# Layer 0 without Sqrt and with one set of ScalarE functions asked for first; layer 1 loads its first image ahead of its weights

## The chip, the core and the metric

The kernel runs on one core of a Trainium2 chip. The metric is the device time of one launch in microseconds (us). TensorE (PE) multiplies matrices, VectorE (DVE), ScalarE (ACT) and GpSimd (POOL) work element by element, SyncE (SP) issues transfers (DMA). Each engine runs its own instructions in the order in which they stand and waits for the others by semaphores. [...] which functions are at hand depends on the set that is loaded, and a load is an instruction of its own in its stream (ACT_TABLE_LOAD in the profile).

## The reference

Four layers, each `x = x + layer(gn(x))` on four images of 64 x 64 points and 128 channels, in fp32. `gn` normalizes groups of 4 channels over an image with `1 / sqrt(var + 1e-5)`. Cut to what matters:

```python
def _gn(v, G=32, eps=1e-5):
    g = v.reshape(B_, H_, W_, G, C_ // G)
    m, s = mean(g), var(g)              # over H, W and the group
    return ((g - m) / jnp.sqrt(s + eps)).reshape(v.shape)
# layer 0: selective scan in four directions
xh, z = split(x @ in_proj_w.T);  z = silu(z)
xc = silu(conv3x3(xh) + conv_b)
delta = softplus(dts + bias);  h = exp(delta * A) * h + delta * u * B;  y = h . C
y = layernorm(y) * z @ out_proj_w.T
# layer 1: Fourier layer
f = irfft(rfft(x, rows)[:16] * w1) + irfft(rfft(x, columns)[:16] * w2)
out = layernorm(relu(f @ ff_w0 + b0) @ ff_w1 + b1)
```

Layer 2 is an attention between Fourier-transformed tokens, layer 3 a windowed attention; neither is touched.

## The kernel before

**Layer 0** (`layer0`, line 83). For each image `before` (line 148) reads it twice in 8 chunks of 512 points: first for the statistics of the group norm (`bn_stats`, line 161, then `group_scale`, lines 64 to 80), then to transpose it (`x_ps`, line 183), normalize it (`xn`), project it to `z` (`zp`, line 198, two matmuls) and convolve it as 9 taps each for two halves of the channels (`cv`, line 206). Each result goes through `silu` (line 217): ScalarE takes Exp of the negated value, Ln of one plus that, Exp of the negated result, and DVE multiplies with the value itself (`e`, line 222), which frees its PSUM bank; four banks go round. The result is written to DRAM, and the convolved one a second time in the order of columns (`xw`, lines 231 to 234). For the first image this runs alone, as an opening; for the next three it is a side work, spread over the scan of the image before.

The scan goes over 128 units (4 images, 4 directions, 8 chunks). A unit has 16 slots, one a state: GpSimd makes `dB` (line 477), ScalarE the decay `dA` (Exp, line 483) for two halves, DVE scans them (`h`, line 484), TensorE transposes `h` (line 371), ScalarE copies it (line 381), TensorE multiplies it with C (line 406). `inputs` (line 294) makes the next unit's `delta`: Exp (line 320), Ln (line 321), a bound on DVE (line 323), and then `du` on GpSimd (line 326). Inside the scan the order of the engines' instructions is that of the program, written out by hand (`manual_schedule`, line 449); outside of it a scheduler orders them.

**Square roots.** `rstd` (line 43) is Sqrt on ScalarE and a reciprocal on DVE. Layer 0 calls it once an image, from `group_scale`, and asks for the set with Exp and Ln behind it (`exp_and_ln`, lines 121 and 164); for the layer norm at its end (`after`, lines 250 to 254) it takes Exp(-0.5 Ln(var + eps)). That request has no data to wait for: outside of the hand-written order it stands at the head of the ScalarE stream as built, not behind the Sqrt.

**Layer 1** (`layer1`, line 716) loads its weights (`layer1_weights`, line 586): `w1` and `w2` on SyncE's queue, 2 MB each, six small ones on ScalarE's, `c_an1` the fifth of them. Then it runs one image after another (`layer1_image`, line 607): the image in four loads of 512 KB (`load_image`, line 709), the group norm's statistics (lines 58 and 59), the row transform with `c_an1` (`pu`, line 631, `U`, line 632), the mixing of modes with `w1` (`pg`, lines 643 and 646), the transform back (`pt`, `ph`), the same along the columns with a second copy of the image (`xa`, line 626) and `w2`, and a two-layer network (`pf`, `po`). Behind its first image the weights of layer 2 are loaded and prepared with short DVE operations (`layer2_weights`, line 732); the scheduler places them among those of the image. Its tiles lie where layer 0's lay, so its loads wait for layer 0's last work.

A DMA reports to one of eight semaphores, shared out in turn over the queues of SyncE and ScalarE, and as built the next DMA on a semaphore is issued only when the one before it has landed.

Of the kernel before, what the change touches and what calls it, by code (L numbers as in the profile page):

```python
# [10 lines left out]
F32 = mybir.dt.float32  # L11
AF = mybir.ActivationFunctionType
# [4 lines left out]
P = 128  # L17
# [3 lines left out]
DM = 128  # L21
NJ = NT // P
# [7 lines left out]
class Shared:  # L30
# [30 lines left out]
                nc.scalar.copy(keep[:, c * CH : (c + 1) * CH], ps)  # L61
        return self.group_scale(st, psum, small, tag)

    def group_scale(self, st, psum, small, tag):
        nc = self.nc
        mv = small.tile([P, 2], F32, name="gn_mv")
        nc.vector.bn_aggr(mv, st)
        gm = psum.tile([P, 1], F32, name="gn_gm", tag=tag)
        nc.tensor.matmul(gm, lhsT=self.gmat, rhs=mv[:, 0:1], start=True, stop=True)
        gms = small.tile([P, 1], F32, name="gn_gms")  # L70
        nc.vector.tensor_copy(gms, gm)
        d = small.tile([P, 1], F32, name="gn_d")
        nc.vector.tensor_tensor(d, mv[:, 0:1], gms, ALU.subtract)
        nc.vector.scalar_tensor_tensor(d, d, d, mv[:, 1:2], ALU.mult, ALU.add)
        gv = psum.tile([P, 1], F32, name="gn_gv", tag=tag)
        nc.tensor.matmul(gv, lhsT=self.gmat, rhs=d, start=True, stop=True)
        s = self.rstd(small, gv, [P, 1], "gn_s")
        o = small.tile([P, 1], F32, name="gn_o")
        nc.vector.scalar_tensor_tensor(o, gms, -1.0, s, ALU.mult, ALU.mult)
        return s, o  # L80


def layer0(sh, A, x_in, x_out, scr):
# [6 lines left out]
    tc, nc = sh.tc, sh.nc  # L90
    with ExitStack() as ctx:
        pool = lambda name, bufs, **kw: ctx.enter_context(tc.tile_pool(name=name, bufs=bufs, **kw))
        wp = pool("l0w", 1)
        tmp = pool("l0tmp", 2)
        small = pool("l0small", 2)
        ps = pool("l0ps", 1, space=PSUM)
        psx = pool("l0psx", 3, space=PSUM)
        psm = pool("l0psm", 1, space=PSUM)
        psy = pool("l0psy", 1, space=PSUM)

        w_in = wp.tile([P, 4, P], F32, name="w_in")
        nc.sync.dma_start(w_in, A["in_proj"].rearrange("i (m d) -> i m d", d=P))
        cols = wp.tile([P, 14], F32, name="cols")
# [14 lines left out]
        for xd in xds:  # L118
            nc.vector.memset(xd, 0.0)
            nc.vector.memset(xd[64:65, :], 1.0)  # L120
        exp_and_ln = lambda: nc.scalar.preload_act_table_set("natural_log_exp_and_others")
        w_out = wp.tile([P, 2, P], F32, name="w_out")
        nc.sync.dma_start(w_out, A["out_proj"].rearrange("(s p) o -> p s o", p=P))

# [23 lines left out]
        def before(b, bank, later):  # L148

            st = small.tile([P, NCH, 6], F32, name="gn_st")
            for c in range(NCH):
                yield "l"
                t = tmp.tile([P, 4, DM], F32, name="xs", tag="t2", bufs=4)
                nc.sync.dma_start(t, tiles(x_in(b)[c * CH : (c + 1) * CH, :]))
                yield "m"
                pt = bank("gn_ps")
                for q in range(4):
                    nc.tensor.transpose(pt[:, q * P : (q + 1) * P], t[:, q, :], sh.ident)  # L160
                later("dve", lambda c=c, pt=pt: nc.vector.bn_stats(st[:, c, :], pt))
            yield "m"
            s_, o_ = sh.group_scale(st, psm, small, "m")
            exp_and_ln()
            for c in range(NCH):
                yield "l"
                r0, r1 = max(8 * c - 1, 0), min(8 * c + 9, 64)
                j0, j1 = r0 // 2, (r1 + 1) // 2
                t = tmp.tile([P, 6, DM], F32, name="xt", bufs=1)
                nc.sync.dma_start(t[:, 0 : j1 - j0], tiles(x_in(b)[j0 * P : j1 * P, :]))  # L170

                xn = tmp.tile([P, 10, 66], F32, name="xn")
                nc.gpsimd.memset(xn[:, :, 0:66:65], 0.0)
                if c == 0:
                    nc.gpsimd.memset(xn[:, 0, :], 0.0)
                if c == NCH - 1:
                    nc.gpsimd.memset(xn[:, 9, :], 0.0)
                for j in range(j0, j1, 3):
                    yield "m"
                    e = min(j + 3, j1)  # L180
                    pt = bank("x_ps")
                    for q in range(j, e):
                        nc.tensor.transpose(pt[:, (q - j) * P : (q - j + 1) * P], t[:, q - j0, :], sh.ident)
                    a, z = max(r0, 2 * j), min(r1, 2 * e)
                    later(
                        "dve",
                        nc.vector.tensor_scalar,
                        xn[:, a - 8 * c + 1 : z - 8 * c + 1, 1:65],
                        pt.rearrange("p (h w) -> p h w", w=64)[:, a - 2 * j : z - 2 * j],
                        s_,  # L190
                        o_,
                        ALU.mult,
                        ALU.add,
                    )
                for s in range(2):
                    yield "z"
                    zp = bank("zp")
                    nc.tensor.matmul(zp, lhsT=w_in[:, 2 + s, :], rhs=xn[:, 1:9, 1:65], start=True, stop=True)
                    silu(zp, 0.0, 0.0, scr(f"z{b % 3}")[s, :, c * CH : (c + 1) * CH], later, (0, 0, 1))
                for s in range(2):  # L200
                    for t in range(9):
                        yield "c"
                        if t == 0:
                            pm = bank("cv")
                        dy, dx = divmod(t, 3)
                        nc.tensor.matmul(  # L206
                            pm,
                            lhsT=taps[:, s, t, :],
                            rhs=xn[:, dy : dy + 8, dx : dx + 64],
                            start=(t == 0),  # L210
                            stop=(t == 8),
                        )
                    bias = conv_b[:, s : s + 1], conv_nb[:, s : s + 1]
                    xo = silu(pm, *bias, scr(f"xr{b % 2}")[s, :, c * CH : (c + 1) * CH], later, (0, 1, 2))
                    later("act0", by_columns, xo, scr(f"xw{b % 2}")[s], c, slots=4)
# [220 lines left out]
        def later(place, f, *a, slots=1, **kw):  # L436

            todo.setdefault((slot + slots, place), []).append(lambda: f(*a, **kw))
# [147 lines left out]
def layer1_weights(sh, A, wp):  # L586
    nc = sh.nc
    w = {}
    for name in ("w1", "w2"):
        w[name] = wp.tile([P, 16, 2, P], F32, name=name)  # L590
        nc.sync.dma_start(w[name], A[name])
    w["ff0"] = wp.tile([P, 4, P], F32, name="ff0")
    nc.scalar.dma_start(w["ff0"], A["ff_w0"].rearrange("i (f k) -> i f k", k=P))
    w["ff1"] = wp.tile([P, 4, P], F32, name="ff1")
    nc.scalar.dma_start(w["ff1"], A["ff_w1"].rearrange("(f k) o -> k f o", k=P))
    w["b0"] = wp.tile([P, 4], F32, name="b0")
    nc.scalar.dma_start(w["b0"], A["ff_b0"])
    w["rows"] = wp.tile([P, 3, P], F32, name="rows1")
    nc.scalar.dma_start(w["rows"], A["l1_rows"].partition_broadcast(P))
    w["an"] = wp.tile([P, 96], F32, name="c_an1")  # L600
    nc.scalar.dma_start(w["an"], A["c_an1"])
    w["sy"] = wp.tile([P, 256], F32, name="c_sy1")
    nc.scalar.dma_start(w["sy"], A["c_sy1"])
    return w


def layer1_image(sh, w, pools, x_dram, x_out):

    nc = sh.nc
    big, tmp, small, ps = pools  # L610
    x = big.tile([P, NJ, DM], F32, name="x1")
    load_image(nc, x, x_dram)
    s_, o_ = sh.group_norm(lambda j: x[:, j, :], ps, small, tag="a")
    o8 = small.tile([P, 1], F32, name="o8")
    nc.vector.tensor_scalar(o8, o_, 8.0, None, ALU.mult)
# [2 lines left out]
    for axis in range(2):  # L618
# [20 lines left out]
        for g in range(4):  # L639
            pg = ps.tile([P, 4, 2, 64], F32, name="pg", tag="b")  # L640
            for q in range(4):
                m = 4 * g + q
# [34 lines left out]
    for c in range(NCH):  # L677
# [14 lines left out]
        st = small.tile([P, 4, 6], F32, name="ln_st")  # L692
# [4 lines left out]
        r = sh.rstd(small, mv[:, :, 1], [P, 4], "ln_r")  # L697
# [11 lines left out]
def load_image(nc, x, x_dram):  # L709
    for q in range(4):  # L710
        nc.sync.dma_start(
            x[:, 8 * q : 8 * q + 8, :], x_dram[1024 * q : 1024 * q + 1024, :].rearrange("(j p) d -> p j d", p=P)
        )


def layer1(sh, A, x_in, x_out, l2w, wt):

    tc, nc = sh.tc, sh.nc
    with ExitStack() as ctx:
        pool = lambda name, bufs, **kw: ctx.enter_context(tc.tile_pool(name=name, bufs=bufs, **kw))  # L720
        pools = pool("l1big", 2), pool("l1tmp", 2), pool("l1small", 2), pool("l1ps", 4, space=PSUM)
        wp = pool("l1w", 1)
        w = layer1_weights(sh, A, wp)
        for b in range(NB):
            layer1_image(sh, w, pools, x_in(b), x_out(b))
            if b == 0:
                setup = pool("l2set", 1)
                later = layer2_weights(sh, A, l2w, setup, pools[3], wt)
        return later
# [1094 lines left out]
```

## Time and profile before

| | |
|---|---|
| time, median of 3 (lowest to highest) | 8356.3 us (8350.7 to 8357.7) |
| span of the profiled run | 8355.5 us |
| busy: PE, DVE, ACT, POOL | 79%, 81%, 76%, 66% |
| opening of layer 0, to the first `du` | 0 to 247.5 us |
| scan and rest of layer 0 | to 6091 us |
| layer 1 | to about 6700 us |
| table loads in layer 0 | 79 of 1283 ns |
| ScalarE in layer 0, the costliest | `dA` 4096 x 690 ns, `hT` 2048 x 1010 ns |
| DVE in layer 0, the costliest | `h` 4096 x 1270 ns |

The page shows the busy share of each engine in 40 slices of 209 us, and the groups of instructions by line, operation and tile, with what ended the idle time before them. The views used below cut out a stretch: the timeline lists instructions in order of time (start, duration, engine, line, operation, out<-in, count, and in brackets the engine's idle time before it with what ended it); the waits sum who waited for whom; the chain of waits follows what ended last back through what released it; the windows give each engine's busy time, TensorE's granted clock and the DMA engines' share and rate in stretches.

### The profile page before, as it was taken

What the parts mean: (1) busy time and instruction counts of PE and PEld (TensorE: products, weight loads), DVE (VectorE), ACT (ScalarE), POOL (GpSimd) and SP (SyncE); (2) the same over time, 40 slices, a digit from 0 to 9 for tenths busy, and PEclk for the clock granted to TensorE, in tenths of its full rate; (3) what the DMA queues carried; (4) which work ended last, traced back from release to release, by engine and by line L of the source; (5) the groups of instructions that cost most, each with busy time, mean ns of one, the idle gap of its engine ahead of it and who ended that gap; (6) DMA issues with size and microseconds to landing.
All of it is one profiled execution on the core that took longest, in us unless ns stands there. A gap on an engine that the chain in (4) does not pass through costs nothing.

```text
span 8355.5 us, 140584 instructions
## 1 busy us (share of the span) xinstructions
PE 6592.1 (79%) x52976; PEld 4182.2 (50%) x52976; DVE 6756.6 (81%) x7952; ACT 6333.0 (76%) x10320; POOL 5485.2 (66%) x2502
## 2 busy tenths in 40 slices
PE   7588888778788777888887777787778978686689
PEld 3344454444445444444544444454457756464456
DVE  2689999998899999889999999999944545645578
ACT  6799999999899889989989999999822213315467
POOL 0689889988888889888888999999800011020233
PEclk9799999999999999999999999999989988788799
DMA  6445555444555554455555445554432041331332
GB/s 111 132 144 179 166 170 173 164 160 156 169 169 177 175 171 153 154 176 159 175 173 175 163 153 181 177 175 169 165 94 52 18 118 38 86 100 31 95 93 78
DMA packets 1281978, 1163.79 MB, mean 139 GB/s; under 512 B 637973, under 2 KB 1075825, under 8 KB 1214354
## 3 DMA queue, kind: packets, MB, share of 16 engines
q1 hardware_dynamic: 1279618, 1153.06, 43.6%
q8 instruction: 417, 6.83, 0.3%
q14 instruction: 263, 2.15, 0.1%
q10 hardware_dynamic: 1680, 1.74, 0.1%
HBM read 962.66 MB, written 189.74 MB: 138 GB/s over the span
## 4 chain that ended last, share of the span: by engine, by line
PE 21%; ACT 11%; DVE 10%; issue 3%; POOL 2%; DMA 2%; SPq 1%; ACTq 0%; DVEq 0%; POOLq 0%
DVE h L484 4%; ACT hT L381 4%; ACT dA L483 4%; PE pt L371 2%; POOL dB L477 1%; PE po L686 1%; PE pf L681 1%; PE pz L872 1%; PE pt L1507 1%; PE pu L872 1%; DVE in_st L872 1%; PE pb L872 1%; PE ps L1561 1%; DVE m L872 1%; PE pa L872 1%
## 5 line engine op out<-in xcount | busy, mean ns | idle before, releaser
L484 DVE TENSOR_TENSOR_SCAN h<-dA,state,dB 128x512 f32<-128x512 f32 x4096 | 4962.0, 1270 | 379.5 <-ACT dA L483 269.8
L477 POOL TENSOR_TENSOR dB<-du,Bb 128x1024 f32<-128x1024 f32 x2048 | 4820.0, 2385 | 567.4 <-DVE h L484 398.0
L371 PE MATMUL pt<-ident,h 128*128 128x128 f32 x16384 | 2256.9, 282 | 1023.1 <-ACT hT L381 1018.9
L371 PEld LDWEIGHTS pt<-ident,h 128*128 128x128 f32 x16384 | 1846.3, 143 | 2063.8 <-ACT hT L381 1815.1
L483 ACT ACTIVATE dA<-delta,A_neg 128x512 f32<-128x512 f32 x4096 | 2745.6, 690 | 157.8 <-DVE h L484 136.7
L381 ACT COPY hT<-pt 128x1024 f32<-128x1024 f32 x2048 | 2068.9, 1010 | 182.5 <-PE pt L371 169.3
L406 PE MATMUL yT<-hT,W 128*32 128x256 f32 x16384 | 1400.9, 415 | 2.7 <-DVE y L422 2.1
L872 POOL COPY XG<-Xs 64x9 f32<-64x9 f32 (+2 forms) x44 | 11.0, 294 | 1024.9 <-ACT Xs L872 1024.9
L406 PEld LDWEIGHTS yT<-hT,W 128*32 128x32 f32 x16384 | 454.3, 150 | 353.6 <-issue 338.4
L206 PE MATMUL cv<-xn,taps 128*128 128x512 f32 x1152 | 620.1, 639 | 8.7 <-DVE e L222 8.7
L1545 POOL TENSOR_TENSOR S<-S,sm 128x784 f32<-128x784 f32 x128 | 191.4, 1495 | 408.2 <-DVE sm L1543 347.3
L317 PE MATMUL dp<-xd,w_dt 65*128 65x512 f32 x512 | 300.0, 669 | 105.4 <-ACT Ct L304 92.0
L326 POOL TENSOR_TENSOR du<-delta,u 128x1024 f32<-128x1024 f32 x128 | 305.1, 2384 | 78.5 <-DVE delta L323 78.5
L206 PEld LDWEIGHTS cv<-xn,taps 128*128 128x128 f32 x1152 | 185.5, 190 | 248.5 <-issue 244.6
L298 PE MATMUL xd_ps<-u,w_x 128*48 128x512 f32 x512 | 251.1, 614 | 44.0 <-DMA u<-l_xw 19.8
L1552 ACT ACTIVATE S<-S,mx 128x196 f32<-128x196 f32 x512 | 227.9, 448 | 32.7 <-DVE mx L1579 32.2
L682 ACT ACTIVATE h<-pf,b 128x512 f32<-128x512 f32 x128 | 88.0, 687 | 145.0 <-PE pf L681 145.0
L323 DVE SCALAR_TENSOR_TENSOR delta<-delta,dp 128x512 f32<-128x512 f32 x256 | 169.3, 661 | 27.7 <-ACT delta L321 27.7
L317 PEld LDWEIGHTS dp<-xd,w_dt 65*128 65x128 f32 x512 | 79.4, 195 | 220.7 <-ACT Ct L304 150.6
L1421 POOL MEMSET kp<- 128x210 f32 (+1 forms) x8 | 1.8, 287 | 275.0 <-DMA x<-m 275.0
L320 ACT ACTIVATE delta<-dp 128x512 f32<-128x512 f32 x256 | 152.4, 595 | 30.1 <-PE dp L317 25.6
L1507 PE MATMUL pt<-ident,S 128*98 128x128 f32 x1024 | 165.2, 285 | 4.4 <-POOL S L1545 1.9
(336 smaller groups left out, 7282.4 us busy)
## 6 DMA issues: line engine op xcount, KB each, us to landing
Bb<-l_B SPq DMA_DIRECT2D x512, 1024.0 KB
W<-l_W SPq DMA_DIRECT2D x512, 256.0 KB
l_y<-y SPq DMA_DIRECT2D x128, 512.0 KB
u<-l_xw SPq DMA_DIRECT2D x64, 512.0 KB
y<-l_y SPq DMA_DIRECT2D x64, 512.0 KB
u<-l_xr SPq DMA_DIRECT2D x64, 512.0 KB
V<-l_v SPq DMA_DIRECT2D x512, 49.0 KB
wr<-wt SPq DMA_DIRECT2D x128, 136.0 KB
```

What stands on the lines that cost most here:

```text
L206: nc.tensor.matmul(pm, lhsT=taps[:, s, t, :], rhs=xn[:, dy : dy + 8, dx : dx + 64], start=(t == 0), stop=(t == 8),)
L298: nc.tensor.matmul(xd_ps, lhsT=w_x[:, s, k, :], rhs=u[:, s, :], start=(s == 0), stop=(s == 1))
L317: nc.tensor.matmul(dp, lhsT=w_dt[:, k, s * P : (s + 1) * P], rhs=xd, start=True, stop=True)
L326: nc.gpsimd.tensor_tensor(du, delta, u, ALU.mult)
L371: nc.tensor.transpose(pt[:, j, s, :], G["h"][:, s, t0 : t0 + 32, :].rearrange("p t n -> p (t n)"), sh.ident)
L381: return lambda: nc.scalar.copy(hT, pt.rearrange("p j s d -> p j (s d)"))
L406: nc.tensor.matmul(U["yT"][e][32 * jo : 32 * jo + 32, qo % 2, :], lhsT=U["Ws"][G["g"]][:, :, 4 * q + j], rhs=hT[:, j, :], start=((e, jo) n ...
L477: nc.gpsimd.tensor_tensor(dB, du, B_now[:, q : q + 1, :].to_broadcast([P, 2, CH]), ALU.mult)
L483: nc.scalar.activation(dA, delta[:, s, :], AF.Exp, scale=A_neg[:, k, s, n : n + 1])
L484: nc.vector.tensor_tensor_scan(h[:, s, :, q], dA, dB[:, s, :], state[:, s, n : n + 1], ALU.mult, ALU.add)
L872: r = f(*args, **kw)
L1507: nc.tensor.transpose(pt[:, half, hp, :], U["S"][:, e, hp, 98 * half : 98 * half + 98], sh.ident)
```

## The change

In layer 0 the square root is replaced by Exp(-0.5 Ln(var + eps)), and the set of functions that has both Exp and Ln is asked for once, ahead of everything else. It is meant to keep ScalarE from switching sets. In layer 1 the first image is loaded ahead of the weights, and the analysis matrix ahead of the other small weights, since the image's statistics and row transform come before the first use of `w1`.

```diff
-    def group_scale(self, st, psum, small, tag):
+    def group_scale(self, st, psum, small, tag, rstd=None):
...
-        s = self.rstd(small, gv, [P, 1], "gn_s")
+        s = (rstd or self.rstd)(small, gv, [P, 1], "gn_s")
...
+        nc.scalar.preload_act_table_set("natural_log_exp_and_others")
         w_in = wp.tile([P, 4, P], F32, name="w_in")
...
-        exp_and_ln = lambda: nc.scalar.preload_act_table_set("natural_log_exp_and_others")
+        def exp_rstd(pool, var, shape, tag):
+            r = pool.tile(shape, F32, name=tag)
+            nc.scalar.activation(r, var, AF.Ln, bias=sh.eps5[: shape[0]])
+            nc.scalar.activation(r, r, AF.Exp, scale=-0.5)
+            return r
...
-            s_, o_ = sh.group_scale(st, psm, small, "m")
-            exp_and_ln()
+            s_, o_ = sh.group_scale(st, psm, small, "m", exp_rstd)
...
 def layer1_weights(sh, A, wp):
     w = {}
+    w["an"] = wp.tile([P, 96], F32, name="c_an1")
+    nc.scalar.dma_start(w["an"], A["c_an1"])
     for name in ("w1", "w2"):
...
-    w["an"] = wp.tile([P, 96], F32, name="c_an1")
-    nc.scalar.dma_start(w["an"], A["c_an1"])
...
-def layer1_image(sh, w, pools, x_dram, x_out):
+def layer1_image(sh, w, pools, x_dram, x_out, x=None):
...
-    x = big.tile([P, NJ, DM], F32, name="x1")
-    load_image(nc, x, x_dram)
+    if x is None:
+        x = big.tile([P, NJ, DM], F32, name="x1")
+        load_image(nc, x, x_dram)
...
+        x = pools[0].tile([P, NJ, DM], F32, name="x1")
+        load_image(nc, x, x_in(0))
         w = layer1_weights(sh, A, wp)
         for b in range(NB):
-            layer1_image(sh, w, pools, x_in(b), x_out(b))
+            layer1_image(sh, w, pools, x_in(b), x_out(b), x if b == 0 else None)
```

## The prediction

> **What bounds the kernel now.** I read the page first (which engine is full in which slice), then the groups of ScalarE for its table loads, then the stretches in which the change lies: the waits and the timeline of layer 0's opening, the timeline of its first scan units, the chain of waits across the change of layer. ACT and DVE are at 8 to 9 tenths from slice 2 to slice 28, so layer 0 from about 250 to 6090 us is paced by the two of them together; before it comes an opening of 250 us, and behind it a stretch in which nothing computes.
>
> The groups of instructions, whole kernel, the rows of the table loads (count | busy us, mean ns | idle before):
>
> ```profile
> L342 ACT ACT_TABLE_LOAD x55 | 70.6, 1283 | 1.0
> ...
> L46 ACT ACT_TABLE_LOAD x8 | 10.3, 1283 | 20.4 <-DMA c_sy<-in_c_sy 20.3
> L321 ACT ACT_TABLE_LOAD x8 | 10.3, 1283 | 0.1
> L483 ACT ACT_TABLE_LOAD x8 | 10.3, 1283 | 0.1
> L121 ACT ACT_TABLE_LOAD x4 | 5.1, 1283 | 0.8 <-PEq L1814 0.7
> ```
>
> Layer 0 holds 79 of these loads (55 + 8 + 8 + 4, and 4 of L46). By windows, 61 lie before 250 us, 18 after: so they cluster where layer 0 opens. The timeline there (start, duration, engine, line, operation, idle before):
>
> ```profile
> 101.22 0.69 ACT L342 ACTIVATE e<-cv,conv_nb 128x512 f32<-128x512 f32 x1
> ...
> 101.92 1.28 ACT L342 ACT_TABLE_LOAD   x1
> ...
> 103.21 0.63 ACT L342 ACTIVATE e<-e 128x512 f32<-128x512 f32 x1
> 103.86 1.28 ACT L342 ACT_TABLE_LOAD   x1
> 105.15 0.63 ACT L342 ACTIVATE e<-e 128x512 f32<-128x512 f32 x1
> 105.81 0.75 DVE L222 SCALAR_TENSOR_TENSOR e<-cv,cols,e 128x512 f32<-128x512 f32 x1 [3.46 <-ACT e L342]
> ...
> 106.71 3.44 PE L206 MATMUL cv<-xn,taps 128*128 128x512 f32 x4 [2.31 <-DVE e L222]
> ```
>
> One silu is Exp, load, Ln, load, Exp, then the product on DVE, which frees the PSUM bank; TensorE waits 2.31 us for that bank. And its first four matmuls then take 0.86 us each, against 14.76 us for 34 (0.43 each) in the chunk before: the wait costs a second time, as a slow clock. The waits of PE from 33 to 250 us:
>
> ```profile
> PE cv L206 <- DVE e L222: 8.7, 4, 2.3
> PE zp L198 <- DVE xn L342: 8.5, 8, 1.8
> PE zp L198 <- DVE e L222: 5.5, 3, 1.8
> ```
>
> So 8.7 + 5.5 = 14.2 us of the opening hang on the silu, 8.5 on something else (xn). In the first scan units (timeline from 268 us) the same pair of loads stands in front of a dA:
>
> ```profile
> 282.43 1.28 ACT L321 ACT_TABLE_LOAD   x1
> ...
> 284.38 1.28 ACT L483 ACT_TABLE_LOAD   x1
> 285.67 0.69 ACT L483 ACTIVATE dA<-delta,A_neg 128x512 f32<-128x512 f32 x1
> ...
> 286.39 1.29 DVE L484 TENSOR_TENSOR_SCAN h<-dA,state,dB 128x512 f32<-128x512 f32 x1 [4.61 <-ACT dA L483]
> ```
>
> Last, the chain of waits from 6080 to 6290 us, where layer 1 begins:
>
> ```profile
> 6097.14 8.71 DMA pa<-in_pa
> 6105.86 6.13 SPq L711
> 6112.04 5.38 SPq L711
> ...
> 6117.46 10.96 DMA x<-x
> ...
> 6133.69 9.54 PE pu L631 x64
> ```
>
> The image is the last to arrive (6128.43), behind w1 and w2, and pg, the first user of w1, starts only at 6144.21.
>
> [...] from the Exp that ends at 101.91 to the Ln that starts at 103.21 a load costs 1.30 us in all, which I use as 1.29. [...] between 401 and 1828 us Exp and Ln alternate with no load. [...] w2's issue waited 9.0 us for b0, a transfer of a few bytes from the ACT queue, which went beside w1's 2 MB.
>
> **The change part by part.**
>
> *Opening of layer 0.* With Sqrt gone and the set asked for ahead of all, nothing in layer 0 needs another set; as built, layer 0 has 1 load in place of 79, and every other instruction of it keeps its place except that a Reciprocal on DVE (0.16 us) becomes an Exp on ACT (about 0.18, as L254's row of the same kind), for four small columns: nothing. Each silu gets 2 x 1.29 = 2.57 us shorter. The largest wait is 2.31, so the bank is free before TensorE asks: with the loads gone, the product would end near 103.9, and PE reaches that cv at 102.41 + 1.99 = 104.4. All 14.2 us go. The four chunks that wait at cv also run slowly: 17.4 us for 36 cv matmuls against 14.76 + 1.02 = 15.8 undisturbed; 4 x 1.6 = 6.4. After the last cv nothing hides the last silu: 2.6. Then the first delta: Exp, load, Ln, DVE, twice in sequence, where the second L483 load of each pair lies beside a matmul or GpSimd's du; 2 x 1.29 = 2.6. Sum 25.8. The waits for xn (8.5) stay. What could take the place: the slots of e and xw. A column write xw takes 7.8 us to land (issued 101.34, ACT freed at 109.16); in the faster rhythm z's second Exp would ask for that slot about as late relative to the write as now, so at most 1 us, off PE's path.
>
> *First scan units.* Six pairs of L321 and L483 loads remain past 250 us. Before 286.39 DVE idles 4.61 us, 2.57 of it the two loads in sequence. As a test: the unit from 290.2 to 341.4 us and the one from 341.4 to 391.8 (two pairs each; from the starts of du) take 51.2 and 50.4 us, those at 493.0, 539.2 and 584.1 take 46.2, 44.9 and 46.0: 5 us for two pairs, the whole price. 6 x 2.57 = 15.4; I take 15.
>
> *The three later group norms* (400, 1834, 3313 us): the load of Sqrt's set lies in ACT's wait for gn_gv (3.3 to 5.1 us) and is free; the one behind Sqrt delays the next dA by 1.3, but the gain is cut by DVE's own gn_o (1.13 us beside GpSimd): 1.0 + 0.7 + 0.7 = 2.4; I take 2.
>
> *Start of layer 1.* Image first, then w1, w2. Its first load takes w1's place at 6093.75. Its third waits for the analysis matrix c_an, now first on the ACT queue, its fourth for ff1, by the semaphores of the build. Before the fourth lands some 3.2 MB must pass: x 2.1, ff0 and ff1 0.5, rows 0.2, c_sy and c_an 0.2, pa and pb 0.3. The next image of the same form ran at 281 to 312 GB/s (windows 6142 to 6148). 3.2 MB at 290 is 11 us from 6095: landed at 6106, against 6128.4. Bounds: x alone, 2.1 MB at 290 and 1 us: 6103; all 3.2 MB at 177 GB/s, the rate beside xa: 6113. From there on the chain is the same length: 5.3 us to gn_s, 10.5 to pg. pg at 6122 finds w1 landed: 2.5 MB more at 385 GB/s (window 6096 to 6098) is 6112.5; in the slow case 6113 + 8 = 6121 against pg at 6129. w2 at 6118, xa (at 177 GB/s, 12 us) at 6130, while its pu comes at 6165 - 22 = 6143. So 22 us. DVE's constants for layer 2 move behind the first axis' hT copies: 13 short operations, some 6 us, in the 7 us of the second pu, so U at L635 is just met; cost 0, at worst 1. The first waits for tok, landed near 6139 and asked for at 6146.
>
> Sum: 25.8 + 15 + 2 + 22 = 65 us; 8356.3 - 65 = 8291.
>
> **The rivals.** (1) *The first layer's gain shrinks to a half*: the 512 B packets of x run at 177 GB/s or tok holds up DVE, and layer 1 wins 10, not 22: 8303. For it: x's own issues took 6.1 and 5.4 us; against: they stood behind w2. 12%. (2) *Transfers become the bound of the opening*: the column writes are many and small, the DMA engines are at 0.54 to 0.72 there; if waits for slots take back 14 + 6, only 5 remain there: 8311. Against it: 3.0 us of such waits in all now. 8%. (3) *Slower*: the scan's units are no steady clockwork (44.9 to 46.2 for like ones); if the shifted phase of ACT against GpSimd and DVE cost 0.7 us in each of 120 units, 84 us, more than the gain: 8375. Nothing in the trace speaks for it but that spread. 2%. (4) *More*: x lands at 6103, PE stays at full clock through pu: 8281. 8%.
>
> **How the numbers follow.** The main case, 70%, with its own bounds (layer 1 15 to 25, opening 21 to 28, units 13 to 16) lies in 8282 to 8303. Rival 1 and half of rivals 2 and 4 are taken in: 8280 to 8312. Faster by over 0.2% (16.7 us) in all cases but (3) and a mixture of (1) and (2): 0.96; same 0.02; slower 0.02.
>
> **What would show it.** One table load before 6090 us; PE's waits for e gone from 33 to 250 us, the waits for xn still near 8; first du near 222 in place of 247.5; units 1 and 2 near 46 us; x landed some 12 us after its first issue, in place of 24 (and 35 after w1's), and pg 16 us later without a wait for w1. Wrong if the waits for e become waits for transfers, if the units stay at 50, or if pg waits for w1.

## The result and the profile after

| | before | after |
|---|---|---|
| time, median (lowest to highest, runs) | 8353.5 us (8348.6 to 8357.7, 4) | 8298.5 us (8295.9 to 8301.2, 4) |
| span of the profiled run | 8355.5 us | 8299.4 us |
| table loads | 99 | 21 |
| first `du` | 247.5 us | 220.7 us |
| last `du` of layer 0 | 5998.3 us | 5949.4 us |
| first `pg` of layer 1 | 6144.2 us | 6087.0 us |

After over before is 0.9934, with a 95% interval from 0.9917 to 0.9952: 55 us faster, where 65 were forecast. A second pair on another chip gave 0.9936 (0.9924 to 0.9949).

The table loads among the groups of ScalarE in the kernel after (count | busy us, mean ns | idle before): one is left for all of layer 0, that of L102; the others belong to the later layers.

```profile
L883 ACT ACT_TABLE_LOAD x12 | 15.4, 1283 | 48.7 <-DVE in_d L883 48.5
L46 ACT ACT_TABLE_LOAD x4 | 5.1, 1283 | 25.9 <-DMA x<-x 25.8
L1563 ACT ACT_TABLE_LOAD x4 | 5.1, 1283 | 0.1
L102 ACT ACT_TABLE_LOAD x1 | 1.3, 1283 | 0.7 <-PEq L1825 0.7
```

The timeline of the opening shows a silu without loads. From Exp to the product on DVE it takes 2.04 us (87.85 to 89.89), 4.59 before (101.22 to 105.81), and TensorE goes on with `cv` under it without a gap:

```profile
83.79 11.75 PE L214 MATMUL cv<-xn,taps 128*128 128x512 f32 x27
...
87.85 0.69 ACT L350 ACTIVATE e<-cv,conv_nb 128x512 f32<-128x512 f32 x1 [4.09 <-PE cv L214]
...
88.57 1.29 ACT L350 ACTIVATE e<-e 128x512 f32<-128x512 f32 x2
...
89.89 0.75 DVE L230 SCALAR_TENSOR_TENSOR e<-cv,cols,e 128x512 f32<-128x512 f32 x1 [5.41 <-ACT e L350]
```

The waits of PE from 33 to 230 us (us in total, times, longest): the two rows that ended at `e` are gone, the one for `xn` is what it was, and no wait for a transfer has come in. The first row, the wait for the last column write, was 19.8 us before and is not new.

```profile
PE xd_ps L306 <- DMA u<-l_xw: 16.8, 1, 16.8
PE zp L206 <- DVE xn L350: 8.6, 8, 1.9
```

In the first scan units the pair of loads between delta and `dA` is gone, and DVE's idle time ahead of the scan falls from 4.61 to 0.31 us:

```profile
294.88 0.60 ACT L328 ACTIVATE delta<-dp 128x512 f32<-128x512 f32 x1
...
295.51 0.64 ACT L329 ACTIVATE delta<-delta 128x512 f32<-128x512 f32 x1
...
296.04 0.68 ACT L491 ACTIVATE dA<-delta,A_neg 128x512 f32<-128x512 f32 x1
...
296.75 1.28 DVE L492 TENSOR_TENSOR_SCAN h<-dA,state,dB 128x512 f32<-128x512 f32 x1 [0.31 <-ACT dA L491]
```

At the change of layer the chain of waits of the kernel after looks different from what was forecast:

```profile
6046.53 6.54 DMA ff<-in_ff_w
6053.08 18.46 DMA x<-x
6071.69 1.95 PE gn_ps L58 x8
...
6076.82 9.24 PE pu L640 x64
...
6087.04 0.69 PE pg L652 x2
```

The image's last quarter, 512 KB, is issued at 6053.08 and lands 18.46 us later, in place of 10.96 us. From the issue of the first quarter (6045.39) it is 26.2 us, where the forecast had some 12. That is where most of the missing time is. `w1`, as forecast, is no wait.

### The profile page after: what moved, and what is told of

The parts are those of the page before. It is cut to its first block, busy times and chain, and to the rows that moved or that the text cites. A ratio compares the mean times of both kernels' runs of the same rounds, so it can differ in the third digit from the quotient of the medians.

```text
span 8299.4 us, 140501 instructions
## 1 busy us (share of the span) xinstructions
PE 6571.5 (79%) x52976; PEld 4171.0 (50%) x52976; DVE 6753.8 (81%) x7948; ACT 6229.0 (75%) x10246; POOL 5482.7 (66%) x2502
## 3 DMA queue, kind: packets, MB, share of 16 engines
q10 hardware_dynamic: 1680, 1.74, 0.1%
## 4 chain that ended last, share of the span: by engine, by line
PE 21%; ACT 11%; DVE 11%; issue 3%; DMA 2%; POOL 2%; SPq 1%; DVEq 0%; ACTq 0%; POOLq 0%
DVE h L492 4%; ACT hT L389 4%; ACT dA L491 4%; PE pt L379 2%; PE po L695 1%; PE pf L690 1%; POOL dB L485 1%; PE pz L883 1%; PE pu L883 1%; PE pt L1518 1%; DVE in_st L883 1%; PE pb L883 1%; DVE m L883 1%; PE pa L883 1%; PE ps L1572 1%
## 5 line engine op out<-in xcount | busy, mean ns | idle before, releaser
L691 ACT ACTIVATE h<-pf,b 128x512 f32<-128x512 f32 x128 | 88.0, 687 | 146.7 <-PE pf L690 146.7
L329 ACT ACTIVATE delta<-delta 128x512 f32<-128x512 f32 x256 | 162.3, 634 | 8.1
```

## The experiments

Single times of one kernel lie up to 27 us apart, and the part behind layer 1's last transform, which no kernel here changes, took 1765 to 1780 us in the profiles. So each kernel is also read by its trace, between marks that stand close to the change: the starts of `du`, the first `pg`, and the start of the last `pu` group of layer 1. That group is the column transform of the last image; one of the expectations below calls it the last row transform. Beside each time stands the kernel before on the same chip.

**Each part alone.** The first kernel has the new layer 0 and the old order of loads in layer 1, the second the reverse:

```diff
 # layer 0 alone
-        x = pools[0].tile([P, NJ, DM], F32, name="x1")
-        load_image(nc, x, x_in(0))
         w = layer1_weights(sh, A, wp)     # c_an1 fifth again
-            layer1_image(sh, w, pools, x_in(b), x_out(b), x if b == 0 else None)
+            layer1_image(sh, w, pools, x_in(b), x_out(b))
 # layer 1 alone
-            s_, o_ = sh.group_scale(st, psm, small, "m", exp_rstd)
+            s_, o_ = sh.group_scale(st, psm, small, "m")
+            exp_and_ln()
```

> The change to layer 0 alone; layer 1 loads in its old order. Theory A (the traces' account: layer 0 gave 48 us, layer 1 only 8 to 9): 48 below before, 8305 to 8307, and the first layer-1 image lands some 35 us after the weights' first issue, as before. Rival B (the forecast's split, layer 0 43 and layer 1 22, with some 10 us lost further on): 43 below before, 8310.

> The change to layer 1 alone; layer 0 keeps Sqrt and its 79 loads. Theory A: 8 to 9 below before, 8344 to 8346. Rival B: 22 below before, 8331.

Layer 0 alone: 8312.1 against 8359.7 us, 0.9943 (0.9930 to 0.9955), 48 us. Layer 1 alone: 8352.4, 0.9994 (0.9986 to 1.0002), 5 us by the ratio, not to be told from none. By the trace, from the last `du` to the first `pg`, layer 1 alone takes 138.2 us, as the changed kernel does (137.6), and layer 0 alone 146.7 against 145.9 before. The times of layer 0 alone fit both accounts; those of layer 1 alone leave no room for 22 us, and the trace agrees. So theory A of these two runs holds: the new order of loads is worth some 8 us up to `pg`, not 22.

**Do the weights hold the image up?** The first guess (theory A of the next two runs) was that the weights' 16 KB packets take turns with the image's packets of 512 B. One kernel makes `w1` and `w2` wait until the image has landed, another was to give them packets of 512 B:

```diff
 # weights wait for the image
         w[name] = wp.tile([P, 16, 2, P], F32, name=name)
+        nc.gpsimd.tensor_copy(w[name][:, 0, 0, 0:1], x[:, NJ - 1, 0:1])
         nc.sync.dma_start(w[name], A[name])
 # rows apart
-        w[name] = wp.tile([P, 16, 2, P], F32, name=name)
+        wide = wp.tile([P, 16, 2, P + 8], F32, name=name)
+        w[name] = wide[:, :, :, :P]
         nc.sync.dma_start(w[name], A[name])
```

> The changed kernel, with w1 and w2 each issued only when the last quarter of the first image has landed (GpSimd copies one column of that quarter into the tile first; the load then overwrites it). Theory A (the weights' 16 KB packets take turns with the image's 512 B packets, so that the last quarter drips): that quarter lands 4 to 6 us after its issue near 6053, so near 6058 in place of 6071.5; pg starts 6 to 13 us earlier, limited by w1, which now begins near 6059; time 8286 to 8293. Rival C (the image is late by the waits for c_an and ff1 and by the small weights on ScalarE's queue, w1 and w2 matter little): the quarter lands near 6068 to 6071 still, w1 behind it, pg waits for w1; time 8300 to 8310.

> The changed kernel with w1 and w2 in tiles whose rows are 136 elements apart, so that they arrive in packets of 512 B, as the image does, in place of 16 KB; order and bytes as in the changed kernel. Theory A (one packet of each transfer in turn, so the big packets take the share): the image's last quarter lands 8 to 13 us earlier, 6058 to 6064; w1 later; time 8288 to 8296. Rival C: it lands within 2 us of 6071.5; time 8297 to 8303. If the bytes count and not the packets, also no change.

With `w1` and `w2` held back until 6072.72 the last quarter still took 17.36 us (chain of waits, first fence), so theory A fell: no 16 KB packet was under way. (The first half of `xa`, next in SyncE's queue, took their place, in packets of 512 B.) The windows (us, busy time and count of PE, PEld, DVE, ACT, POOL, clock, DMA share, GB/s) show what did go on:

```profile
6054.94 17.36 DMA x<-x
```

```profile
6062.00:6066.00 4.00, 1.34 (x7) 1.37 (x8) 0.22 (x1) 1.17 (x1) 0.00 (x0) 0.50 1.12 138
6066.00:6072.00 6.00, 0.60 (x3) 0.20 (x1) 1.18 (x2) 0.12 (x1) 0.00 (x0) 0.50 0.28 85
```

In the last 6 us before the quarter landed the DMA engines were busy for 0.28 of their time, 4.5 of 16, at 85 GB/s. The author read this as work on few of them. But for those of 4 B, the records of packets in that stretch show two kinds only: 512 B on SyncE's queue and 2048 B on ScalarE's, and the latter are the rows of six arrays for layer 2 (pa, pb, vra, vrb, via, vib, each 68 rows of 2 KB). Time: 8295.3 against 8359.7, 0.9923 (0.9910 to 0.9937). Rival C had the landing nearly right (6072.3; it said 6068 to 6071), and its 8300 to 8310 and its wait of `pg` for `w1` were missed.

With the rows apart the quarter took 16.08 us, and 8308.3 us, 0.9937 (0.9925 to 0.9950). But the records show packets of 8 KB for the weights, not of 512 B: the edit did not make what it was meant to make, and on the size of packets this run says nothing.

**The six arrays.** The 0.28 above is the time of 4.5 engines. The packet records name no engine, but they can be summed: in the changed kernel from 6060 to 6066 us `w1`'s packets fill the time of 12.1 engines, and those of the image and the arrays together that of 4.5. From 6060 to 6068 the records have 45 to 50 packets of 512 B and as many of 2 KB in each 2 us, one for one. From 6060 to 6066 a 512 B packet took 58 ns on average and a 2 KB one 136; from 6046.0 to 6049.7, before the arrays start, a 512 B packet took 30. So theory D, the author's estimate from these sums: the image's last quarter is done early on some 12 engines, which go on to `w1`, and drips on the other 4 or so, where the arrays lie too. Test: move the six to SyncE's queue, behind the image and the weights; and, to see whether fewer arrays cost less, leave two of them.

```diff
 # all six
-        return load(name, [Q, 32, 16], A[name], setup, nc.scalar)
+        return load(name, [Q, 32, 16], A[name], setup)
 # four of six
+        return load(name, [Q, 32, 16], A[name], setup, nc.scalar if name in ("pa", "pb") else nc.sync)
```

> The changed kernel with the six arrays of 68 rows for layer 2 (pa, pb, vra, vrb, via, vib) moved from ScalarE's queue, where they were issued beside the image, to SyncE's queue behind the image, w1, w2 and xa. Theory D (these arrays, 68 packets of 2 KB each, lie on a few of the 16 DMA engines and take turns there with the image's last quarter, while the other engines have gone on to w1): that quarter lands 4 to 7 us after its issue in place of 18.5; from the last du of layer 0 to the first pg 124 to 129 us in place of 137.6; time 8285 to 8291. Theory A (w1's 16 KB packets hold the image up): still 16 to 18 us, 137, 8298. What could take the gain: DVE's work on these arrays comes later and stands in front of the image's own DVE work; then 8298 or more.

> As e5, but pa and pb stay on ScalarE's queue, ahead of the last quarter's issue; only vra, vrb, via and vib move. If the image's packets and those of the arrays take turns one by one on the few engines that have the arrays, two arrays delay the last quarter by about half of what six did: it lands 9 to 12 us after its issue (18.5 with six, 8.0 with none), and from the last du to pg it is 127 to 132 us. If any of them is enough: 16 us and 135.

The chain of waits with all six moved:

```profile
6050.67 3.68 DMA c_an<-in_c_an
6054.36 7.97 DMA x<-x
...
6069.30 10.03 PE pu L640 x64
...
6080.31 0.69 PE pg L652 x2
```

and with four moved:

```profile
6047.05 10.98 DMA x<-x
...
6075.66 0.69 PE pg L652 x2
```

In both chains the piece `x<-x` is the third quarter: 16 `gn_ps` stand behind it, and the fourth has landed before they are through. The issues and semaphore updates in the traces give both quarters:

| arrays beside the image | third: issue to landing | fourth: issue to landing | first issue to last landing | last `du` to `pg` |
|---|---|---|---|---|
| six (changed kernel; second profile) | 11.8; 11.8 us | 18.5; 18.6 us | 26.2; 26.3 us | 137.6; 139.8 us |
| two | 11.0 us | 9.3 us | 16.9 us | 128.6 us |
| none | 8.0 us | 9.1 us | 13.5 us | 126.5 us |

Theory D holds in its effect: without the arrays the last quarter takes half the time (9.1 us in place of 18.5) and `pg` comes 11 us sooner. That the arrays lie on few engines was not shown by itself. Fewer arrays cost less, but not as expected. Two hold up the third quarter, by 3.0 us, and no longer the fourth: their last packets start at 6057.4 us, before the third lands at 6058.0. Six hold up the fourth too, by 9.4 us. An estimate comes near: if the 68 packets of each array are spread over the 4.5 engines of the sums above, 15 on each, then at the 111 and 122 ns that a 2 KB packet took (means with two and with six) two arrays are 3.4 us and six 11.1; the whole image took 3.4 and 12.7 us longer than with none. (With none the fourth quarter is issued 0.5 us after the third, otherwise 3.5 to 3.9, so a part of these 3.4 and 12.7 may be that.) That the 0.8 MB matter by more than their bytes follows from the rate: 0.8 MB at the 317 GB/s of the kernel with none, from 6054.4 to 6062.4, would be 2.6 us, and the last quarter's time fell by 9.4.

The 4 to 7 us expected for the last quarter without the arrays were missed, the 9 to 12 us with two met. Times: 8300.3 against 8363.1, 0.9923 (0.9911 to 0.9936), where 8285 to 8291 was expected, and 8295.5 against 8356.1, 0.9924 (0.9910 to 0.9939). Of the first gap 10 us is the chip, on which the kernel before too was slower by that. By the times alone neither is told from the changed kernel.

**The waits for c_an and ff1, and a better version.** Layer 1's own small weights follow to SyncE's queue as well; only the image and `c_an1` are asked for at first:

```diff
-    w["ff0"] = ...; nc.scalar.dma_start(...)    # also ff1, b0, rows, sy
+    # on nc.sync: w1, then sy, w2, ff0, ff1, b0, rows
-        return load(name, [Q, 32, 16], A[name], setup, nc.scalar)
+        return load(name, [Q, 32, 16], A[name], setup)
```

> As the run before, and layer 1's own small weights (ff0, ff1, b0, rows, c_sy) too on SyncE's queue, behind w1 or w2: only the image and c_an are asked for at first. If the waits for c_an and ff1 before the third and fourth quarters cost time of their own: the last quarter is issued near 6049 in place of 6053 and lands near 6053 to 6055; from the last du to pg 120 to 124; time 8281 to 8287. If not, because the DMA engines are full in any case: as the run before, within 2 us.

> The kernel of e6 once more, beside the changed kernel. Its first pg came 17.8 us earlier after the last du than in the changed kernel, and the last row transform of layer 1 some 13 us earlier: 12 to 18 us under the changed kernel of this call. If the later layers take it back: the same within 4 us.

> The changed kernel once more, to stand on the same chip beside the runs of this call. All theories: 0.992 to 0.995 of before; from the last du to the first pg 136 to 140 us.

```profile
6048.60 7.45 DMA x<-x
...
6060.19 8.87 PE pu L640 x64
...
6070.04 0.68 PE pg L652 x2
```

In this chain the piece `x<-x` is the last quarter. It is issued 98.4 us after the last `du` (103.7 in the changed kernel, 101.0 with the six arrays moved) and lands at 6056.05. From the last `du` to `pg` it is 119.8 us, in the second run of this kernel 121.2, against 126.5 with the six arrays alone moved and 137.6 and 139.8 in the changed kernel. So the small weights of layer 1 cost 5 to 7 us of their own up to `pg`. The edit takes away both the waits for `c_an1` and `ff1` and the small weights' traffic beside the image: the last quarter is issued 2.6 to 2.9 us sooner and takes 1.6 us less, and the two were not parted further. Up to the last column transform of layer 1, 573.6 against 588.1 us remain in the pair on one chip, 14.5 of the 18.6. Times: 8290.8 (8281 to 8287 expected) against 8363.1 before, 0.9913 (0.9900 to 0.9927); and on the chip that ran both, 8292.8 against 8310.5 of the changed kernel and 8356.1 of before. By the time alone, the intervals against before (0.9906 to 0.9931, and 0.9924 to 0.9949) overlap; the trace parts them. Its times are the lowest here.

**What a load costs in the scan.** The kernel before with the alternation ended at the first `dA` of the scan, so that only the six pairs in the units go:

```diff
+                    if i == 0 and n == 0:
+                        once = small.tile([P, 1], F32, name="once")
+                        nc.scalar.activation(once, delta[:, 0, 0:1], AF.Sqrt)
+                        exp_and_ln()
```

> The kernel before with one Sqrt of a single column behind the first dA of the first scan unit and the request for the set behind it, so that the six pairs of loads in the first three units are gone and those of the opening stay (it adds 2 loads and 0.3 us there; the column is not used). By the forecast's term: units 1 and 2 near 46 us, the first near 40; 12 us net, 8341 to 8345. By the traces: units 1 and 2 at 43.2 as in the changed kernel, the first near 39; 15 to 18 us net, and some 2 to 4 of it given back in units 3 to 5: 8339 to 8345. The first du stays at 247 to 248.

Time 8343.0 against 8363.1, 0.9975 (0.9967 to 0.9984), 21 us. Starts of `du`, the first four of the scan (us), and the units between them:

```
before              247.5  290.2  341.4  391.8     42.7  51.2  50.4
layer 1 alone       248.0  290.7  341.9  393.1     42.7  51.2  51.2
this kernel         246.0  281.0  324.2  367.3     35.0  43.2  43.1
after               220.7  257.4  300.5  343.7     36.6  43.2  43.2
```

So units 1 and 2 go to 43.2, not to 46. The three units give 23 us for 12 loads, 1.9 us a load and not 1.28. A likely reason can be read from the windows of unit 1, before and after (columns as above):

```profile
290.20:341.40 51.20, 37.38 (x278) 22.28 (x277) 41.16 (x38) 45.42 (x65) 39.92 (x19) 0.87 0.40 141
```

```profile
257.40:300.50 43.10, 32.48 (x278) 19.56 (x276) 40.89 (x38) 40.02 (x61) 39.89 (x18) 1.00 0.48 167
```

With the loads TensorE's granted clock is 0.87 in the unit, without them 1.00. Before the `pt` at 328.00 us TensorE has waited 4.38 us for `hT` behind the first pair of loads, and before the same `pt` in the kernel after 1.68 us. From 325.5 to 335.7 us the clock is granted at 0.5, and the work runs at half rate, in the timeline of before:

```profile
330.92 2.08 PE L317 MATMUL dp<-xd,w_dt 65*128 65x512 f32 x2
...
332.79 1.91 PE L371 MATMUL pt<-ident,h 128*128 128x128 f32 x8
```

and in that of after:

```profile
293.72 1.12 PE L325 MATMUL dp<-xd,w_dt 65*128 65x512 f32 x2
...
294.68 1.04 PE L379 MATMUL pt<-ident,h 128*128 128x128 f32 x8
```

How much of the 0.6 us a load this clock makes was not measured by itself.

The absence of Sqrt is not enough; the request is needed too. This kernel has neither Sqrt nor the request:

```diff
-        nc.scalar.preload_act_table_set("natural_log_exp_and_others")
```

> The changed kernel without the request for the set: no Sqrt in layer 0, but as built 849 loads in place of 21, the two sets alternating for Exp and Ln through the whole scan. If a load costs its 1.29 us wherever ScalarE paces: two pairs a unit as in units 1 and 2 before, 5 to 8 us for each of some 126 units, and 174 loads ahead of yg at up to 1.3: 630 to 1200 us more than the changed kernel, 8930 to 9500. If loads hide in ScalarE's waits once the scan runs: below 8450.

9753.6 us against 8363.1, 1.1664 (1.1643 to 1.1686), above the expected range. Its groups of ScalarE:

```profile
L490 ACT ACT_TABLE_LOAD x333 | 427.2, 1283 | 6.0
L328 ACT ACT_TABLE_LOAD x256 | 328.4, 1283 | 4.6
...
L445 ACT ACT_TABLE_LOAD x174 | 223.2, 1283 | 3.1
```

1455 us more than the 8298.5 of the changed kernel (1443 more than its 8310.5 on a third chip) for 828 loads more: 1.74 to 1.76 us each, close to the 1.9 of the units and again above 1.28. The mean granted clock was 0.854, 0.946 in the kernel after. On average nothing of a load hides in ScalarE's waits. So taking Sqrt out is worth nothing without the request. The reverse, asking first and keeping Sqrt in the opening, was not run.

**The later group norms.**

```diff
-            s_, o_ = sh.group_scale(st, psm, small, "m", exp_rstd)
+            s_, o_ = sh.group_scale(st, psm, small, "m", exp_rstd if b == 0 else None)
+            if b:
+                nc.scalar.preload_act_table_set("natural_log_exp_and_others")
```

> The changed kernel with Sqrt and a request for the set behind it for images 1 to 3 of layer 0, as before, and the new form for image 0 alone: 27 loads as built in place of 21. By the forecast's term for the three later group norms 2 us slower than the changed kernel, so not to be told from it by the time; by the trace the unit with the group norm is 0.7 to 1.3 us longer. If a load in the scan costs what it does without the request (1455 us for 828 loads): 1.8 us a load, up to 10 us.

8309.8 against 8310.5 of the changed kernel on the same chip, 0.9932 (0.9918 to 0.9946) of before. The unit with the first of these norms, from the fourth `du` to the fifth, took 52.7 us here, 50.9 to 53.3 in nine other profiles with the new form, and the last `du` came at 5951.0 against a mean of 5950.6 (5946.0 to 5958.8). The term of 2 us is not to be seen either way, and nothing speaks for a cost of 10 us.

## Why the prediction was right, and where its parts were wrong

The means over the profiles of all kernels that share a stretch, against the forecast's terms (us):

| term | forecast | measured | from |
|---|---|---|---|
| opening | 25.8 | 25.9 | first `du` 247.8 (2 profiles) to 221.9 (10) |
| first units | 15 | 22.4 | first `du` to the fourth: 144.7 to 122.3 |
| later group norms | 2 | -1.7 | fourth `du` to the last: 5604.8 to 5606.5, each spread over some 4 to 11 |
| start of layer 1 | 22 | 7.2 | last `du` to `pg`: 146.2 (3) to 139.0 (5) |
| behind `pg` | 0 | -2.6 | `pg` to the last column transform of layer 1: 445.8 (3; 444.0 to 448.2) to 448.4 (5; 447.1 to 448.9) |
| sum | 64.8 | 51.2 | |

The 51 compare with 55 and, by the second pair's ratio, 53 us of the times.

- **Opening: right in mechanism and size.** One load in place of 61, TensorE's waits for `e` gone and with them the slow clock at `cv` (granted 0.55 from 106.7 to 110.2 us before, 1.00 from 50 to 190 us after; 36 matmuls in 15.6 us, 17.4 before), the waits for `xn` still 8.6, no wait for column writes in their place. Rival 2, transfers as the new bound, had nothing.
- **First units: the mechanism was right, the term mis-sized.** It was "5 us for two pairs", read from a comparison with units of 46 us. Those units carry the silus and convolutions of the next image; units 1 and 2 carry only transposes for its statistics. Undisturbed they take 43.2, so the two pairs cost 7 to 8. One of the readings was off besides: the unit from 584.1 takes 49.3 us to the next `du` at 633.4, not 46.0; at 630.1 stands only the semaphore instruction ahead of it. The comparison took a different kind of unit for a like one, and hid the cost of a load above its own 1.28 us.
- **Later group norms**: 2 us were forecast, and not to be told from none.
- **Start of layer 1: the step that failed** is "Before the fourth lands some 3.2 MB must pass ... at 290 is 11 us"; it was 26.2 us from the first issue. The step took the bytes ahead of the quarter and one total rate. Two arrays were in the sum as 0.3 MB and the other four were left out. With the six beside it the last quarter took 9.4 us longer than with none, while the total rate looks full: the changed kernel moves 287 GB/s from 6057 to 6071.5, nearly the 290 assumed, but most of it is the weights (3.3 of 4.2 MB, 12.1 engines' time). That the quarter waits behind the arrays on the 4 or so engines left is the author's estimate from the packets' times. The rival with a layer 1 of 10 us named another cause (slow 512 B packets of the image); its number was near, its cause not the one shown. The waits for `c_an1` and `ff1`, which the forecast named but did not price, and the small weights' traffic cost 5 to 7 us more up to `pg`, as the run that takes both away shows.
- **Behind pg** the forecast held that "from there on the chain is the same length". The order of TensorE as built is not the same: before, the first column transform starts when 16 of the `ph` matmuls are through; after, behind all 32. Timelines of PE, before and then after:

```profile
6160.91 3.72 PE L661 MATMUL ph<-c_sy,GT 128*128 128x256 f32 x16
6164.46 0.82 PE L655 MATMUL pt<-ident,G 128*128 128x128 f32 x6
6165.12 0.58 PE L631 MATMUL pu<-c_an,xa 128*128 128x96 f32 x4
```

```profile
6103.74 3.72 PE L670 MATMUL ph<-c_sy,GT 128*128 128x256 f32 x16
6107.30 0.82 PE L664 MATMUL pt<-ident,G 128*128 128x128 f32 x6
6108.41 3.72 PE L670 MATMUL ph<-c_sy,GT 128*128 128x256 f32 x16 [0.29 <-ACT GT L666]
6111.97 6.28 PE L640 MATMUL pu<-c_an,xa 128*128 128x96 f32 x55
```

But the order by itself costs next to nothing up to the first `pg` of the columns, which waits for that transform (chains of waits, before and then after):

```profile
6176.96 0.69 PE pg L643 x2
```

```profile
6120.25 0.69 PE pg L652 x2
```

From the first `pu` (6133.55 and 6076.68) that is 43.4 and 43.6 us. In all it is 43.2 to 43.7 us in the three profiles with the old order of loads, and 45.4 to 46.1 in the four others with the new one. What makes these 2 us, and the 2.6 at the end of layer 1, where the spreads of the two groups overlap, stays open.

So the time lay 7 us above the 8291 of the forecast, and not further off, because an overestimate of 15 us in layer 1 met an underestimate of 7 in the units. The direction and the largest term stood on the profile; the closeness of the sum is partly luck. Of the signs that the forecast named, units near 46 us and an image landed some 12 us after its first issue did not come (43.2 and 26.2); the others did.

## What to carry to other kernels

Price a table load where it stands: those of the three later group norms, which lay in or near a wait, were not to be seen in the time, while in a pipeline whose ScalarE and VectorE are at 8 to 9 tenths a load cost 1.7 to 1.9 us, more than its own 1.28, and the granted clock of TensorE was lower with the loads (0.87 against 1.00 in the unit, 0.854 against 0.946 over the kernel). When a transfer is moved ahead, sum the packets' times of its neighbours and not only their bytes: six arrays of 68 rows on another queue (0.8 MB, 2.6 us at 317 GB/s) held a 512 KB load up by 9.4 us while the total rate, 287 GB/s, looked full. And compare a unit of work only with units that carry the same side work.

## What the runs showed of the hardware that was not expected

- Arrays of 68 rows and the rest of a load beside them took the time of about 4.5 of 16 DMA engines (share 0.28 at 85 GB/s), while `w1` filled the time of 12.1 in the changed kernel. There 512 B packets of one queue went one for one with 2 KB packets of the other (147 and 138 from 6060 to 6066 us), at 58 and 136 ns on average.
- With Exp and Ln alone in layer 0 and no request for the set that has both, the build alternates between two sets, 849 loads in place of 21, at 1.74 to 1.76 us of the kernel's time each.
- Rows of 512 B that lie 544 B apart in SBUF were still moved in packets of 8 KB by the records (209 packets of 8 KB or more from 6050 to 6066 us), where the source was contiguous.
